# Dealing the work of a fused cross-attention block anew: when one batch ends and the next begins

## The chip, the cores and the metric

The kernel runs on one core of one Trainium2 chip. The metric is the device time of one execution in microseconds (us), and the median of several executions is compared. A profile of one execution gives the rows that are read below; times in it count from the start of its span.

## The reference

For each of 4 batches (512 query rows, 512 context rows, width 512, 16 heads of 32), in float32:

```
x1 = layer_norm(x) * ln1_w + ln1_b
q, k, v = x1 @ q_w + q_b,  ctx @ k_w + k_b,  ctx @ v_w + v_b
a = softmax(q k^T / sqrt(32) + mask) v          # per head
h = a @ cproj_w + cproj_b + x
y = layer_norm(h) * ln2_w + ln2_b
out = h + gelu(y @ fc_w + fc_b) @ proj_w + proj_b   # inner width 2048
```

## The kernel before

**Blocks.** Attention is cut into 16 windows w (batch w // 4, a group of four heads w % 4) and each window into two halves of 256 queries: 32 blocks, numbered p = 2w + half. The same number names the pair (w, half) whose weights block p computes. `block` (L277) does for one block: `scores` (L252: 8 matmuls, one for each head and query tile, into 8 PSUM banks), `soften` (L259: for each of the 8, VectorE adds the mask and takes the minimum, L263, then ScalarE takes the exponential and its sum, L267), four 32x32 transposes by VectorE (`turn`, L275, into the tile tb), and one of the reciprocal sums (L298).

**Copies.** The transposed weights have to change partitions. `copies` (L319) does it with 16 DMAs (L331) of SyncE, whose queue is SP's, from tb to a target: the one tile pT, or gt or xe for the pairs in IN_G (1, 3, 5, 7) and IN_XE (25, 27, 29, 31) while those lie idle. `exchange` (L312) issues them in order of the pairs as soon as the target is free; tb has two buffers.

**Product with V.** `attend` (L334) multiplies by V: 16 small matmuls (L348), then VectorE multiplies by the reciprocal sums into oT (L353), and the target is free again. The table `due` (L1012) says which pairs are attended ahead of each block: mostly pair p - 2 ahead of block p; ahead of block 9 pairs 6 and 7.

**Filling.** TensorE gets other work between the steps of a block. `put(p, ...)` lists it for block p, and `fill(0)`, `fill(1)` and `fill(2)` in `block` run it: the first two run items as long as their given cost fits into one chain (CHAIN, L835), the third runs what is left. Items of cost 0 run along. So the order on every engine is written out by hand in lines 957 to 1010. The items:

- `A(w)`: the chains for k, q and v of window w (L210, L220, L231); each loads the weights of window w + 2 (L208, SP's queue) when its matmuls are issued.
- `inputs(b)`: x1, load x of batch b into four tiles "xn" (L174); x2, its layer norm (`ln1`, L176, in three parts: two of statistics on VectorE, the last of normalization); x3, its four transposes (`ln_turn`, L151); x4, load the context (L169).
- `C(b)`: the output projection c, four chains (L388), each added to the residual by VectorE (L389). The residual of batch 0 stays on the chip.
- `stat`, `rs`, `norm`, `turns2`: statistics (L125), the reciprocal root on GpSimd (L133), normalization (L143 on ScalarE for batch 0 and for x of batches 1 and 2, L147 on VectorE else) and transposes of the second layer norm. For batch 0 the normalized rows go into new "xn" tiles; that pool has four buffers, so x of a batch and the normalized rows of another take turns.
- `some(n)`: the next n chains of the MLP of batches 0 and 1. For batch 0 two chains of fc (y @ fc_w) are one item, `fc_by_pair` (L545), 14 matmuls (L497) by a 7-product scheme on sums of blocks; a chain of the last projection (`proj`, L554) has four matmuls (L556) and one add on VectorE (L560). Each frees weight slots, and `load_mlp` (L439) issues the next loads (L446).

PSUM has 8 banks, taken in turn by everything above; a matmul group waits until the bank's former content has been read. After block 31 the remaining chains, the last two products, c of batch 3 and then the MLP of the other batches run (`last_mlps`, L592).

Of the kernel before, what the change touches and what calls it, by code (L numbers as in the profile page):

```python
# [50 lines left out]
def xattn_block(ctx: ExitStack, tc: tile.TileContext, x, encT, mask, q_w, k_w, v_w, c_w, fc_w, p_w, vecs, rows, out):  # L51
# [65 lines left out]
    def acc_tile(name):  # L117
        return banks[-1].tile([P, D], F32, tag="acc", name=name)
# [9 lines left out]
    def ln_rs(key):  # L128

        ve = small.tile([P, NT], F32, tag="ve", name=f"ve{key[0]}_{key[1]}")  # L130
        nc.gpsimd.tensor_scalar(ve, S["mv", key][:, :, 1], EPS, 1.0, ALU.add, ALU.mult)
        rs = small.tile([P, NT], F32, tag="rs", name=f"rs{key[0]}_{key[1]}")
        nc.gpsimd.tensor_tensor(rs, ve, nhalf, ALU.pow)  # L133
        S["rs", key] = rs
        if key in NORM_ACT:
            nm = small.tile([P, NT], F32, tag="nm", name=f"nm{key[0]}_{key[1]}")
            nc.gpsimd.tensor_tensor(nm, S["mv", key][:, :, 0], rs, ALU.mult)
            nc.gpsimd.tensor_scalar(nm, nm, -1.0, 0.0, ALU.mult, ALU.add)
            S["nm", key] = nm
# [70 lines left out]
    def prep_k(w):  # L210
        b, g = divmod(w, NG)
        kT = k_q(w, 0)
        acc = acc_tile(f"acck_{w}")
        for d in range(ND):
            nc.tensor.matmul(acc, S["wk", w][:, d, :], eT[:, d, :], start=(d == 0), stop=(d == ND - 1))  # L215
        load_w(w + 2, names=("wk",))
        nc.scalar.activation(kT, acc, AF.Identity, bias=vec[:, KB + g : KB + g + 1], scale=1.0)
        S["kT", w] = kT

    def prep_q(w):  # L220
        b, g = divmod(w, NG)
        qT = k_q(w, 1)
        acc = acc_tile(f"accq_{w}")
        for d in range(ND):
            nc.tensor.matmul(acc, S["wq", w][:, d, :], xT[:, d, :], start=(d == 0), stop=(d == ND - 1))  # L225
        load_w(w + 2, names=("wq",))

        nc.scalar.activation(qT, acc, AF.Identity, bias=qb[:, g : g + 1], scale=-scale)  # L228
        S["qT", w] = qT

    def prep_v(w):  # L231
        b = w // NG
        v = five.tile([P, NT, P], F32, tag="v", name=f"v_{w}")
        acc = acc_tile(f"accv_{w}")
        for t in range(NT):
            for d in range(ND):
                nc.tensor.matmul(  # L237
                    acc[:, ts(t, P)], eT[:, d, ts(t, P)], S["wv", w][:, d, :],
                    start=(d == 0), stop=(d == ND - 1),
                )  # L240
        load_w(w + 2, names=("wv",))
        nc.scalar.copy(v, acc.rearrange("p (t f) -> p t f", t=NT))  # L242
        S["v", w] = v
        if w:
            v_bias(w)
# [62 lines left out]
    def target(w, half):  # L308
        pair = 2 * w + half
        return "gt" if pair in IN_G else "xe" if pair in IN_XE else "pT"  # L310

    def exchange():  # L312

        while waiting and target(*waiting[0]) not in held:
            w, half = waiting.pop(0)
            held[target(w, half)] = w, half
            copies(w, half)
# [16 lines left out]
    def attend(w, half):  # L334

        b, g = divmod(w, NG)
        if g == 0 and half == 0:
            S["oT", b] = one.tile([P, NG, L], F32, tag="oT", name=f"oT_{b}")
        v, pT = S["v", w], S["pT", w, half]
        av = acc_tile(f"av_{w}_{half}")  # L340
        o = S["oT", b][:, g, ts(half, 2 * P)]
        shape, kw = "p (a i q) -> p a i q", dict(a=2, i=NI)
        pv = pT[:, :, :PW].rearrange("p i (a t h q) -> p t h a i q", a=2, t=NT, h=HG)
        p = [[pv[:, t, h] for h in range(HG)] for t in range(NT)]
        r = pT[:, :, PW:].rearrange("p i (a q) -> p a i q", a=2)
        for t in range(NT):
            for h in range(HG):
                nc.tensor.matmul(  # L348
                    av[ts(h, HD), : 2 * P].rearrange(shape, **kw), v[:, t, ts(h, HD)], p[t][h],
                    start=(t == 0), stop=(t == NT - 1),  # L350
                )
        o, a = o.rearrange(shape, **kw), av[:, : 2 * P].rearrange(shape, **kw)
        nc.vector.tensor_tensor(o, a, r, ALU.mult)  # L353
        del held[target(w, half)]
        exchange()
# [24 lines left out]
    def c_bias(b):  # L380
        for t in range(NT):
            add_row(S["h", b, t], 0)
# [25 lines left out]
    def stat2(b, t):  # L408
        ln_stat((2, b), t, S["h", b, t])

    def norm2(b, t):
        h = S["h", b, t]
        y = tiles.tile([P, D], F32, tag="xn", name=f"xn2_{b}_{t}") if stays(b, t) else h
        S.setdefault(("yn", b), {})[t] = y
        ln_norm((2, b), t, y, h)

    def proj_bias(b):
        for t in range(NT):
            if stays(b, t):
                add_row(S["hid", b, t], 1)  # L420
# [32 lines left out]
    def sub(o, x0, x1, engine=None):  # L453
        (engine or nc.vector).tensor_tensor(o, x0, x1, ALU.subtract)  # L454
# [16 lines left out]
    def y_blocks(b):  # L471
        return [S["yT", b][:, 2 * k : 2 * k + 2, j * HL : (j + 1) * HL] for k in range(2) for j in range(2)]

    def y_sums(b):
        y11, y12, y21, y22 = y_blocks(b)
        e = nc.vector if b else nc.gpsimd
        sub(ys[:, 0], y12, y11)
        sub(ys[:, 1], y22, ys[:, 0])
        sub(y12, y22, y12, e)
        sub(ys[:, 2], y21, ys[:, 1], e)  # L480
# [356 lines left out]
    def do(fn):  # L837
        return [(0.0, fn)]

    def A(w):  # L840
        if w >= NW:
            return []
        return [
            (CHAIN, lambda: prep_k(w)),
            (CHAIN, lambda: prep_q(w)),
            (CHAIN, lambda: prep_v(w)),
        ]

    def C(b):
        return [(CHAIN, lambda t=t: cproj(b, t)) for t in range(NT)]  # L850
# [4 lines left out]
    def turns2(b):  # L855
        return [(TURN, lambda d=d: ln2_turn(b, d)) for d in range(ND)]
# [9 lines left out]
    def inputs(b):  # L866
        ln = [(0.0, lambda part=part: ln1(b, part)) for part in range(3)]
        return do(lambda: load_x(b)), ln, turns1(b), do(lambda: load_enc(b))
# [36 lines left out]
    x1, x2, x3, x4 = inputs(1)  # L905
# [14 lines left out]
    def some(n):  # L920
        taken = []
        while n > 0:
            n -= 1 if mlp[0][0] == CHAIN else 2
            taken.append(mlp.pop(0))
        assert n == 0
        return taken
# [4 lines left out]
    def h_(b, *ts_):  # L931
        return do(lambda: load_h(b, *ts_))

    def cb(b):
        return do(lambda: c_bias(b))

    def pb_(b):
        return do(lambda: proj_bias(b))

    def rs(b):  # L940
        return do(lambda: ln_rs((2, b)))

    def stat(b, *ts_):
        return do(lambda: [stat2(b, t) for t in ts_])

    def norm(b, *ts_):
        return do(lambda: [norm2(b, t) for t in ts_])
# [3 lines left out]
    def put(p, *work, before=()):  # L951

        work = [item for part in work for item in part]
        ahead[p] = list(before)
        fills[p] = work
# [5 lines left out]
    k6, q6, v6 = A(6)  # L961
# [4 lines left out]
    put(4, x3[:2], [k5], x3[2:])  # L966
    put(5, [v5, q4])
    put(6, [q5, k6])
    put(7, [v6, q6], cb(0))

    x1, x2, x3, x4 = inputs(2)
    k, q, v = A(7)
    c, t2 = C(0), turns2(0)
    put(8, x1, [k, q, v], x2[:1], x4)
    put(9, c[:1], x2[1:2], c[1:2], x2[2:], stat(0, 0), c[2:3], stat(0, 1), c[3:], stat(0, 2, 3), rs(0))
    k, q, v = A(8)
    put(10, [k], do(fc_sums), x3, [v], t2, do(lambda: y_sums(0)), [q], before=norm(0, 0, 1, 2, 3))
    put(11, some(2), pb_(0), some(2))

    k, q, v = A(9)  # L980
    x1, x2, x3, x4 = inputs(3)
    put(12, [k, q], some(2))
    put(13, some(2), [v], x1)
    k, q, v = A(10)
    put(14, [k, q], x2[:1], some(2))
    put(15, x2[1:2], some(2), [v])

    k, q, v = A(11)
    put(16, h_(1, 0, 1), x2[2:], [k, q], x3[:2], some(2), x3[2:3])
    put(17, [v], x3[3:], h_(1, 2, 3), x4, cb(1), C(1))  # L990
    k, q, v = A(12)
    put(18, [q], some(2), [k])
    put(19, some(2), [v])
    k, q, v = A(13)
    put(20, [k, q], some(2))
    put(21, some(2), [v])
    k, q, v = A(14)
    t2 = turns2(1)
    put(22, [k, q], stat(1, 0, 1, 2, 3), rs(1), some(2), norm(1, 0, 1, 2, 3))
    put(23, some(1), [v], t2, pb_(1), some(1), h_(2, 2, 3, 0, 1))  # L1000
    k, q, v = A(15)
    c = C(2)
    put(24, [k, q], cb(2), [v])
    put(25, c)
    put(26, some(2))
    put(27, some(3))
    put(28, some(3))
    put(29, some(3))
# [1 line left out]
    put(31, some(3))  # L1010

    due = {p: (p - 2,) for p in range(10, 2 * NW)}  # L1012
    due |= {p: (p - 3,) for p in range(3, 9)} | {9: (6, 7)}
    for p in range(2 * NW):
        w, half = divmod(p, 2)
        if half == 0 and w and w % NG == 0:
# [23 lines left out]
    c = C(B - 1)  # L1040
# [49 lines left out]
```

## Time and profile before

| | us |
|---|---|
| median of 3 runs | 802.29 |
| lowest and highest | 801.79, 803.43 |
| the profiled execution | 800.17 |
| its span, first to last instruction | 798.2 |
| TensorE busy in it | 779.3 |
| VectorE, ScalarE, GpSimd busy | 614.2, 331.7, 145.1 |

In the rows PE is TensorE's matmul, DVE is VectorE, ACT ScalarE, POOL GpSimd, SPq the DMA-issuing queue of SyncE. A row of the timeline has start, length, engine, line, operation, out<-in, how many instructions were merged, and in brackets the idle time before it and what ended it. On PE each float32 matmul shows as two instructions, so a chain of 4 has x8. Blocks start with their scores (L257): block 8 at 115.94, block 9 at 136.70, block 10 at 155.41, block 11 at 180.64, block 16 at 262.78, block 26 at 433.72, block 28 at 463.09.

### The profile page before, as it was taken

The numbers are of one execution on the slowest core, as the hardware profiler recorded it, in microseconds if no ns is written. First come the engines' busy times: TensorE is split into PE (matmuls) and PEld (weight loads), VectorE is DVE, ScalarE is ACT, GpSimd is POOL, SyncE is SP. The second block draws the span as 40 slices with busy tenths as digits, with TensorE's granted clock in tenths as the row PEclk, the third lists the DMA queues.
The fourth block names the chain that finished last, engine by engine and source line by source line (L and its number), as shares of the span: only waits on it lengthen the run. The fifth ranks groups of instructions, "written<-read, shape, count | busy, mean of one in ns | idle before, by whom it ended". The sixth has DMA issues, their size and how long they took to land.

```text
span 798.2 us, 12709 instructions
## 1 busy us (share of the span) xinstructions
PE 779.3 (98%) x4394; PEld 514.0 (64%) x4394; DVE 614.2 (77%) x1252; ACT 331.7 (42%) x750; POOL 145.1 (18%) x163
## 2 busy tenths in 40 slices
PE   9999998989999999999999989999999999999998
PEld 6555554456665655556654344445888889988897
DVE  3789895958797966769967958838787999779863
ACT  2577753475773545547544457600310321012200
POOL 1210021235120040100231000120041004400052
PEclk9999999989999999999999999999999999999999
DMA  9988889646797876688668789784442330022001
GB/s 331 295 247 239 218 232 258 185 120 179 198 238 178 253 218 183 165 219 207 163 158 242 201 236 229 205 247 142 159 159 84 94 123 18 28 80 80 14 14 40
DMA packets 60960, 137.20 MB, mean 172 GB/s; under 512 B 12464, under 2 KB 15664, under 8 KB 60768
## 3 DMA queue, kind: packets, MB, share of 16 engines
q1 hardware_dynamic: 59472, 132.43, 60.2%
q0 software_dynamic: 896, 2.82, 1.1%
q10 hardware_dynamic: 528, 1.14, 0.6%
q8 instruction: 35, 0.57, 0.3%
q14 instruction: 29, 0.24, 0.1%
HBM read 58.22 MB, written 6.82 MB: 81 GB/s over the span
## 4 chain that ended last, share of the span: by engine, by line
PE 74%; SPq 10%; DVE 9%; DMA 2%; issue 2%; ACT 2%; DVEq 0%; ACTq 0%
PE q L497 17%; SPq L331 9%; PE accp L556 9%; PE r L645 7%; PE accc L388 7%; PE av L348 6%; PE sc L257 6%; PE acck L215 5%; PE accq L225 4%; PE accf L538 3%; PE accv L237 3%; DVE ptt L263 3%; PE q4p L682 2%; DVE tb L275 2%; PE tp L156 1%
## 5 line engine op out<-in xcount | busy, mean ns | idle before, releaser
L267 ACT ACTIVATE ptt<-ptt,mn 128x512 f32<-128x512 f32 x256 | 181.6, 710 | 138.5 <-DVE mn L263 138.3
L263 DVE CUSTOM_DVE_ANT_0 ptt<-sc,mb 128x512 f32<-128x512 f32 x256 | 161.5, 687 | 22.4 <-PE sc L257 17.7
L275 DVE STREAM_TRANSPOSE tb<-ptt 128x1024 f32<-128x1024 f32 x128 | 154.7, 1220 | 10.8 <-ACT ptt L267 8.7
L556 PE MATMUL accp<-pbt,gt 128*128 128x512 f32 x192 | 85.3, 597 | 0.0
L497 PE MATMUL q<-yT,gt 128*128 128x256 f32 x320 | 79.0, 380 | 0.8 <-DVE pbt L389 0.8
L257 PE MATMUL sc<-pbt 32*128 32x512 f32 x512 | 74.4, 625 | 1.4 <-ACT pbt L228 0.8
L497 PEld LDWEIGHTS q<-yT,gt 128*128 128x128 f32 x320 | 60.8, 190 | 9.7 <-DVE pbt L389 1.6
L556 PEld LDWEIGHTS accp<-pbt,gt 128*128 128x128 f32 x192 | 35.7, 190 | 47.2 <-issue 40.3
L237 PEld LDWEIGHTS accv<-ptt,xe 128*128 128x128 f32 x512 | 59.1, 192 | 7.7 <-issue 3.3
L515 ACT ACTIVATE ga<-ga,vec 128x512 f32<-128x512 f32 x40 | 26.7, 714 | 88.4 <-DVE ga L457 88.4
L497 PE MATMUL q<-ys,gt 128*128 128x256 f32 x240 | 61.7, 380 | 0.0
L237 PE MATMUL accv<-ptt,xe 128*128 128x128 f32 x512 | 60.1, 276 | 0.4 <-DMA ptt<-v_w_dram 0.4
L225 PE MATMUL accq<-xe,ptt 128*128 128x512 f32 x128 | 59.0, 604 | 0.0
L215 PE MATMUL acck<-xe,ptt 128*128 128x512 f32 x128 | 58.7, 602 | 0.0
L388 PE MATMUL accc<-wc,oT 128*128 128x512 f32 x128 | 55.8, 594 | 0.0
L249 POOL TENSOR_TENSOR v<-v,row 128x512 f32<-128x512 f32 x16 | 20.4, 1275 | 178.8 <-ACT v L242 178.8
L348 PE MATMUL av<-pT,v 128*32 128x256 f32 x768 | 46.4, 382 | 5.7 <-DMA xe<-tb 3.0
L257 PEld LDWEIGHTS sc<-pbt 32*128 32x128 f32 x512 | 28.6, 188 | 34.7 <-issue 20.0
L497 PEld LDWEIGHTS q<-ys,gt 128*128 128x128 f32 x240 | 45.6, 190 | 6.5 <-DVE gt L454 0.4
L267 ACT ACTIVATION_READ_ACCUMULATOR ptt<-ptt,mn 128x1 f32 x256 | 47.8, 187 | 0.0
L388 PEld LDWEIGHTS accc<-wc,oT 128*128 128x128 f32 x128 | 24.1, 190 | 30.7 <-issue 27.7
L225 PEld LDWEIGHTS accq<-xe,ptt 128*128 128x128 f32 x128 | 24.2, 195 | 30.4 <-issue 25.7
(180 smaller groups left out, 1094.8 us busy)
## 6 DMA issues: line engine op xcount, KB each, us to landing
pT<-tb SPq DMA_DIRECT2D x384, 136.0 KB, 2.4
pbt<-p_w_dram SPq DMA_DIRECT2D x40, 256.0 KB, 3.5
gt<-fc_w_dram SPq DMA_DIRECT2D x40, 256.0 KB, 2.6
gt<-tb SPq DMA_DIRECT2D x64, 136.0 KB, 2.9
xe<-tb SPq DMA_DIRECT2D x56, 136.0 KB, 2.5
pbt<-fc_w_dram SPq DMA_DIRECT2D x24, 256.0 KB, 3.6
ptt<-k_w_dram SPq DMA_DIRECT2D x16, 256.0 KB, 3.7
xe<-encT_dram SPq DMA_DIRECT2D x16, 256.0 KB, 5.2
```

The source lines that it names most:

```text
L215: nc.tensor.matmul(acc, S["wk", w][:, d, :], eT[:, d, :], start=(d == 0), stop=(d == ND - 1))
L225: nc.tensor.matmul(acc, S["wq", w][:, d, :], xT[:, d, :], start=(d == 0), stop=(d == ND - 1))
L237: nc.tensor.matmul(acc[:, ts(t, P)], eT[:, d, ts(t, P)], S["wv", w][:, d, :], start=(d == 0), stop=(d == ND - 1),)
L257: nc.tensor.matmul(S["sc", w, qt][h], qT[r, ts(qt, P)], kT[r, :], start=True, stop=True)
L263: nc.vector.tensor_tensor_reduce(out=s, in0=S["sc", w, qt][h], in1=S["mb", w // NG], scale=1.0, scalar=FMAX, op0=ALU.add, op1=ALU.min, acc ...
L267: nc.scalar.activation(s, s, AF.Exp, bias=mn, scale=-1.0, accum_out=S["sums", w][:, qt, h : h + 1])
L275: nc.vector.transpose(tv[:, qt % 2, 2 * k : 2 * k + 2], S["ps", w, qt, k])
L331: q.dma_start(out=pT[ts(j, HD), i], in_=tb[ts(i, HD), j])
L348: nc.tensor.matmul(av[ts(h, HD), : 2 * P].rearrange(shape, **kw), v[:, t, ts(h, HD)], p[t][h], start=(t == 0), stop=(t == NT - 1),)
L388: nc.tensor.matmul(acc, S["oT", b][:, g, ts(t, P)], wc[:, g, :], start=(g == 0), stop=(g == NG - 1))
L497: nc.tensor.matmul(o, x[:, k], y[:, k], start=(k == 0), stop=(k == 1))
L556: nc.tensor.matmul(acc, gT[q % 2][:, k, ts(t, P)], S["pw", b, q * FQ + k], start=(k == 0), stop=(k == FQ - 1))
```

## The change

The work stays the same; it is moved between blocks 7 and 26 and the end of attention.

- x of batch 2 is loaded at the end of block 7's work (was at the start of block 8's).
- The product of pair 7, the last of batch 0, is no longer due ahead of block 9; it stands inside block 9, behind v of window 7 (moved there from block 8), the context load and the statistics of x.
- The transposes of x of batch 2 move from block 10 into block 9, between the third and the fourth chain of c. The normalization of batch 0 moves from ahead of block 10 to behind its chains for k and v.
- The first fc pair stands in block 11 behind k and v of window 9, not two pairs alone; blocks 12 to 15 share out q, k and v and the MLP anew. The sum of MLP chains up to block 25 is the same.
- The statistics of batch 1 move from block 22 to blocks 20 and 21, and half of its normalization ahead of the fc pair in block 22.
- Block 26 takes three MLP chains instead of two, so one chain less is left for the end.

```diff
-    put(7, [v6, q6], cb(0))
-
     x1, x2, x3, x4 = inputs(2)
     k, q, v = A(7)
     c, t2 = C(0), turns2(0)
-    put(8, x1, [k, q, v], x2[:1], x4)
-    put(9, c[:1], x2[1:2], c[1:2], x2[2:], stat(0, 0), c[2:3], stat(0, 1), c[3:], stat(0, 2, 3), rs(0))
+    put(7, [v6, q6], cb(0), x1)
+    put(8, [k, q])
+    put(9, [v], x4, x2[:2], do(lambda: attend(3, 1)), c[:1], x2[2:], stat(0, 0), c[1:2], stat(0, 1),
+        c[2:3], stat(0, 2), x3, c[3:], stat(0, 3), rs(0))
     k, q, v = A(8)
-    put(10, [k], do(fc_sums), x3, [v], t2, do(lambda: y_sums(0)), [q], before=norm(0, 0, 1, 2, 3))
-    put(11, some(2), pb_(0), some(2))
-
+    put(10, [k, v], norm(0, 0, 1, 2, 3), do(fc_sums), [q], t2, do(lambda: y_sums(0)))
     k, q, v = A(9)
+    put(11, [k, v], some(2), pb_(0))
+
+    put(12, [q], some(2))
     x1, x2, x3, x4 = inputs(3)
-    put(12, [k, q], some(2))
-    put(13, some(2), [v], x1)
     k, q, v = A(10)
-    put(14, [k, q], x2[:1], some(2))
-    put(15, x2[1:2], some(2), [v])
+    put(13, [k], some(2), [v], x1)
+    put(14, [q], x2[:1], some(2))
+    put(15, some(2), x2[1:2], some(2))
...
-    put(20, [k, q], some(2))
-    put(21, some(2), [v])
+    put(20, [k, q], some(2), stat(1, 0, 1))
+    put(21, some(2), [v], stat(1, 2, 3), rs(1))
     k, q, v = A(14)
     t2 = turns2(1)
-    put(22, [k, q], stat(1, 0, 1, 2, 3), rs(1), some(2), norm(1, 0, 1, 2, 3))
+    put(22, [k, q], norm(1, 0, 1), some(2), norm(1, 2, 3))
...
-    put(26, some(2))
+    put(26, some(3))
...
-    due |= {p: (p - 3,) for p in range(3, 9)} | {9: (6, 7)}
+    due |= {p: (p - 3,) for p in range(3, 9)} | {9: (6,)}
```

## Prediction, on record before the changed kernel ran

> **What bounds the kernel now.** I read the page first, then the stretches of the kernel one by one, then TensorE's instructions in order of time.
>
> ```profile
> PE 779.3 (98%) x4394; PEld 514.0 (64%) x4394; DVE 614.2 (77%) x1252; ACT 331.7 (42%) x750; POOL 145.1 (18%) x163
> ...
> DMA packets 60960, 137.20 MB, mean 172 GB/s; under 512 B 12464, under 2 KB 15664, under 8 KB 60768
> ```
>
> TensorE is busy 98% of the span, so only its idle time, and time in which its matmuls run long, can be won. The view of stretches (PE busy comes first, the granted clock third from the end) shows where that is:
>
> ```profile
> 129.75:139.61 9.86, 7.37 (x81) 3.37 (x81) 3.08 (x9) 0.65 (x2) 1.27 (x1) 0.83 0.90 264
> 155.41:180.64 25.23, 21.75 (x133) 13.77 (x129) 14.56 (x29) 14.62 (x30) 11.38 (x15) 0.86 0.47 119
> 180.64:262.78 82.14, 80.40 (x485) 49.97 (x481) 68.17 (x144) 48.74 (x109) 20.35 (x26) 1.00 0.79 200
> 433.72:463.09 29.37, 26.33 (x140) 11.30 (x137) 23.78 (x51) 12.53 (x34) 1.62 (x3) 1.00 0.82 223
> ```
>
> Two stretches also lose clock. 9.86 us at a mean clock of 0.83 lose 1.7 us and 25.23 us at 0.86 lose 3.5 us, beside 2.5, 3.5, 1.7 and 3.0 us without a matmul in the four. TensorE's rows (start, length, line, and in brackets the idle time before it):
>
> ```profile
> 126.09 3.73 PE L237 MATMUL accv<-ptt,xe 128*128 128x128 f32 x32
> 129.75 1.94 PE L348 MATMUL av<-pT,v 128*32 128x256 f32 x32
> 134.18 2.59 PE L348 MATMUL av<-gt,v 128*32 128x256 f32 x32 [2.49 <-DMA gt<-tb]
> 136.70 2.98 PE L257 MATMUL sc<-pbt 32*128 32x512 f32 x16
> 155.41 2.56 PE L257 MATMUL sc<-pbt 32*128 32x512 f32 x16
> 161.44 1.91 PE L156 MATMUL tp<-ident,xn 128*128 128x128 f32 x16
> 163.19 3.74 PE L237 MATMUL accv<-ptt,xe 128*128 128x128 f32 x32
> 169.75 1.94 PE L156 MATMUL tp<-ident,xn 128*128 128x128 f32 x8 [2.83 <-DVE mn L263]
> 172.34 2.09 PE L156 MATMUL tp<-ident,xn 128*128 128x128 f32 x8 [0.65 <-ACT pbt L217]
> 174.22 4.62 PE L225 MATMUL accq<-xe,ptt 128*128 128x512 f32 x8
> 178.77 1.93 PE L348 MATMUL av<-pT,v 128*32 128x256 f32 x32
> ```
>
> Unhurried work, for the sizes of things:
>
> ```profile
> 203.54 3.60 PE L225 MATMUL accq<-xe,ptt 128*128 128x512 f32 x8
> 206.97 1.89 PE L497 MATMUL q<-yT,pbt 128*128 128x256 f32 x8
> 213.11 1.93 PE L348 MATMUL av<-pT,v 128*32 128x256 f32 x32
> 214.97 2.00 PE L257 MATMUL sc<-pbt 32*128 32x512 f32 x16
> 227.48 1.93 PE L348 MATMUL av<-pT,v 128*32 128x256 f32 x32 [0.70 <-DMA pT<-tb]
> ```
>
> From start to start a chain for q takes 3.43, one fc pair 6.14, a product with V 1.86, scores 1.9 (their 2.00 less the overlap that the other rows have), a chain for v 3.7 (126.09 to 129.75) and 16 transposes 1.75 (161.44 to 163.19). I use 3.5 for a chain of k or of the projections.
>
> **The change, part by part.** *Block 10.* Before, the norms of batch 0 go to ScalarE ahead of the block's exponentials, into tiles that batch 2 still holds until it is transposed:
>
> ```profile
> 163.14 2.93 ACT L143 ACTIVATE xn<-h,nm,rs 128x512 f32<-128x512 f32 x4 [10.82 <-PE tp L156]
> ```
>
> They wait 10.82 us, all exponentials behind them, VectorE behind those, and at last the PSUM banks that the next transposes need: hence the 2.83 us at 169.75 and the slow clock. From 163.19 to 178.77 are 15.6 us for v, 16 transposes and q, worth 3.7 + 1.75 + 3.43 = 8.9: **6.7 us lost**. After, the order of instructions has batch 2's transposes in block 9 and the norms behind block 10's exponentials, k and v. The norms need 2.9 us on ScalarE, which q's 3.43 covers with half a microsecond to spare; if that cover is gone, the transposes wait for the rest, 2.4 us at most. I charge 0.2. The scores at 155.41 ran 0.6 long because VectorE came late from the layer norm's sums; after, it has caught up by then. Together **7.1 gained**.
>
> *Block 9.* Before, the last product of batch 0 follows pair 6's at once and waits 2.49 us for its 16 copies; with the slow clock, 129.75 to 139.61 loses 9.86 - 2 x 1.86 - 1.9 = **4.2 us**. After, k and q end at 126.1, pair 6's product at 128.0, the scores at 129.9 or about 0.5 later (VectorE finishes block 8 at 129.0 and only then frees the last bank), v at 134.1. There the product waits for the same copies. But x of batch 2 is now loaded ahead of them:
>
> ```profile
> 120.73 0.53 SPq L208 DMA_DIRECT2D ptt<-v_w_dram  x1
> 121.85 10.26 SPq L331 DMA_DIRECT2D gt<-tb  x16
> 132.22 1.97 SPq L174 DMA_DIRECT2D xn<-x_dram  x4
> 128.59 0.40 DVE L298 STREAM_TRANSPOSE tb<-rr 128x256 f32<-128x256 f32 x1
> ```
>
> Nothing on SP's queue stood idle there, so the four loads push the copies back by at least their issue, 1.97 us: product at 136.2. The upper end is the other place where the trace has a weight load, x and 16 copies in that order:
>
> ```profile
> 215.56 10.04 SPq L331 DMA_DIRECT2D pT<-tb  x16
> 226.81 0.38 SPq L208 DMA_DIRECT2D ptt<-v_w_dram  x1
> 227.28 1.80 SPq L174 DMA_DIRECT2D xn<-x_dram  x4
> 230.60 11.87 SPq L331 DMA_DIRECT2D pT<-tb  x16
> ```
>
> From 226.81 to the last issue at 242.47 are 15.7 us, and the last copy lands some 2.1 us after its issue (132.11 to 134.18): 17.7. From 120.73 that gives 138.4, and 139.1 with the second weight load that stands here. I take 137.3, between the ends. The wait is then 3.2 us (2.1 to 5.0) instead of 2.5. A wait of that length may cost the clock again, 1.7 us by the first stretch above; a wait that ends at 461.23 shows 3.01 us and clock 1.00, so I charge 1.0. 4.2 - 3.2 - 0.5 - 1.0 = **0.5 lost**.
>
> The Trainium skill (TensorE: Matmul & The Clock Gate, "HAM oscillation — how this bites in real kernels") gives the rule that PE gaps up to about 3.4 us keep the clock. By it this charge would be nothing and the part 0.5 gained. The trace disagrees: after 2.49 and 2.83 us the clock was lost.
>
> *Moved on PE in block 9:* c's first two chains read pair 6's half alone; the third reads pair 7's in its last step, some 10 us after the product. Until then VectorE has the rest of half a block and four stats (3.2 us by the row at 376.72 below) ahead of its multiply; c's first two chains cover that, and what it is later than they are would be idle time. load_enc now follows pair 8's copies; it needs block 10's k, over 10 us later.
>
> *Blocks 11 to 15* have the same chains, dealt anew. The work: five products and scores 18.8, two chains each for k, q and v 21.3, four fc pairs 24.6, four projection chains 14.1, together 78.8 us in the 82.14 of the third stretch, 3.4 lost. After, blocks 12 and 14 hold only q and an fc pair: 1.86 + 1.9 + 3.43 + 6.14 = 13.3 us. There is one pT buffer: copies start when the product before has freed it, and the next product waits for them. Block 13 of before shows that circle at its shortest: 213.11 to 227.48, 14.37 us, with 0.70 idle. So block 12 waits about **1.0**. In block 14 x of batch 3 stands ahead of the copies again: 17.7 us from v's load, issued as v ends, where TensorE needs 13.3: 4.4 waited. At the other end, with the loads landing unseen, the copies need 11.9 from their start (215.56 to 227.48), 2.3 after v: 0.9. I take **2.6**, and 0.9 for the clock; another 0.3 for scores that wait for VectorE. Before hid these loads under k, q and two projection chains. 3.4 - 4.8 = **1.4 lost**.
>
> *Stats of batch 1* go from block 22 to 20 and 21:
>
> ```profile
> 365.06 1.94 PE L348 MATMUL av<-pT,v 128*32 128x256 f32 x32 [0.84 <-DVE tb L275]
> 376.72 0.65 DVE L125 BATCH_NORM_STATS2 st<-h 128x6 f32<-128x512 f32 x1
> 384.09 1.99 PE L257 MATMUL sc<-pbt 32*128 32x512 f32 x14
> 386.26 1.12 PE L257 MATMUL sc<-pbt 32*128 32x512 f32 x2 [0.18 <-DVE oT L353]
> ```
>
> Block 21 is one in which VectorE is late already (0.84 idle). Two stats, 1.7 us of VectorE, go straight onto that (the two at the end of block 20 stand after its last add, in a block of 17 us with room); block 23's scores get back what stats and norms in block 22 cost them: 384.09 to 387.38 are 3.3 us for 1.9 or 2.0, 1.3 too many. **0.4 lost** (0 to 2).
>
> *Block 26* gets a third chain:
>
> ```profile
> 433.72 2.00 PE L257 MATMUL sc<-pbt 32*128 32x512 f32 x16
> 445.84 0.40 DVE L298 STREAM_TRANSPOSE tb<-rr 128x256 f32<-128x256 f32 x1
> 447.65 10.57 PE L556 MATMUL accp<-pbt,gt 128*128 128x512 f32 x24
> 461.23 1.93 PE L348 MATMUL av<-pT,v 128*32 128x256 f32 x32 [3.01 <-DMA xe<-tb]
> ```
>
> Pair 26's copies start when VectorE ends the block, 446.2, whatever TensorE does; its product waits until 461.23. With one chain more (10.57/3 = 3.5) TensorE arrives at 461 instead of 458. The wait goes and a chain is done that stood at the very end: **3.5 gained**. *The end* then has one chain less ahead of the last c:
>
> ```profile
> 553.52 0.69 DVE L389 TENSOR_TENSOR pbt<-accc,pbt 128x512 f32<-128x512 f32 x1 [2.67 <-PE accc L388]
> ```
>
> VectorE has 2.67 us of slack there and loses 3.5: it becomes the one that is late, by about 0.5 with the moved add off its list. **0.5 lost** (0 to 1.5).
>
> Sum: 7.1 - 0.5 - 1.4 - 0.4 + 3.5 - 0.5 = **7.8 us gained**. The profiled execution took 800.17 (span 798.2), 2.1 under the median of the runs, 802.29; I take the gain off the median: **794.5**.
>
> **The rivals.** *No new clock loss* (17%): if the moved waits fall across windows as the one at 461.23 did, 1.9 us come back: **792.6**. For: that row. Against: two of three waits over 2.4 us were hit. The Trainium skill's rule above would give the same time. *Loads hidden* (12%): both lower ends, waits of 2.1 and 0.9, and no clock charge: 1.1 + 1.7 + 1.9 = 4.7 better, **789.8**. Against: DMA share 0.90 in the first stretch. *The norms still wait* (5%), on x of batch 2 or late stats, so block 10 keeps its loss: 7.1 less gained, **801.6**, no change. Against: in the new order the transposes stand a block ahead. *Slower* (10%): the x loads set both waits at the page's mean DMA rate. Four tiles of 512 x 128 numbers of 4 bytes, 1.05 MB, at 172 GB/s are 6.1 us, so block 9's product waits 6.2 and block 14's 7.0, each with two windows of half clock (3.4): 5.4 and 6.9 worse than forecast, **806.8**. Against: 17.7 us for load, x and copies at 226.81. It decides from about 4 us beyond my value at both places.
>
> **How the numbers follow.** Forecast 56%, around 794.5 (790.5 to 799). A measurement of this kernel tells about 0.2%, 1.6 us, from no change. Faster: 56 + 17 + 12 = 85%, less 2 for the upper tail of the forecast: 0.83. Same: the 5 of that rival and 1 of the tail, 0.06. Slower: 10 and 1 of the tail, 0.11. Range 788.5 to 801.5: it leaves out the slower case, half of the unchanged one and a little below.
>
> **What would show it.** Right: ScalarE's norms of batch 0 without a wait, no idle before the transposes of block 10, and under 0.7 us of idle before block 28's product; still 2 to 5 us before pair 7's product, and new idle of 1 and about 2.6 us before the products at the ends of blocks 12 and 14. Wrong: pair 7's product starting later than 139, a wait at the transposes before block 11, more than 1.5 us idle before the first fc pair after c, or another clock loss where none is charged.

## The result and the profile after

| us | before | changed |
|---|---|---|
| median | 802.04 (4 runs) | 796.92 (4 runs) |
| lowest and highest | 801.44, 803.43 | 796.58, 797.56 |
| the profiled execution | 800.17 | 797.24 |
| its span | 798.2 | 795.4 |

The ratio is 0.9935, with a 95% interval of 0.9917 to 0.9952: 5.1 us gained by the medians, 2.9 by the two profiled executions (2.8 by their spans). The forecast was 7.8 us and 794.5.

The changed kernel's view of stretches, for block 9 from its scores on, block 10, blocks 11 to 15, and block 26 up to block 28's product (PE busy first; third from the end the granted clock, the share of its full speed that TensorE's clock had):

```profile
128.88:162.67 33.79, 28.13 (x164) 15.28 (x160) 20.78 (x46) 12.45 (x26) 2.88 (x5) 0.90 0.70 187
162.67:178.85 16.18, 16.18 (x116) 10.09 (x113) 13.08 (x26) 12.18 (x26) 7.64 (x12) 1.00 0.75 187
178.85:263.23 84.38, 79.57 (x485) 49.49 (x481) 68.70 (x146) 51.26 (x111) 24.65 (x29) 1.00 0.78 200
434.07:461.13 27.06, 26.78 (x116) 11.47 (x113) 24.22 (x52) 12.52 (x34) 1.63 (x3) 1.00 0.78 211
```

Block 10 has no idle time and no lowered clock left, and block 26 only 0.28 us. Block 9 carries the loss: 5.66 us without a matmul, and a mean clock of 0.90. TensorE's rows show the same (start, length, line, in brackets the idle time before and what ended it):

```profile
131.12 3.84 PE L237 MATMUL accv<-ptt,xe 128*128 128x128 f32 x32
140.62 3.64 PE L348 MATMUL av<-gt,v 128*32 128x256 f32 x32 [5.66 <-DMA gt<-tb]
144.19 11.51 PE L388 MATMUL accc<-wc,oT 128*128 128x512 f32 x24
155.53 1.91 PE L156 MATMUL tp<-ident,xn 128*128 128x128 f32 x16
...
171.71 3.60 PE L225 MATMUL accq<-xe,ptt 128*128 128x512 f32 x8
175.15 1.91 PE L156 MATMUL tp<-ident,xn 128*128 128x128 f32 x16
...
209.51 1.93 PE L348 MATMUL av<-pT,v 128*32 128x256 f32 x32 [1.26 <-DMA ptt<-q_w_dram]
...
243.64 1.93 PE L348 MATMUL av<-pT,v 128*32 128x256 f32 x32 [3.55 <-DMA ptt<-q_w_dram]
...
461.13 1.93 PE L348 MATMUL av<-pT,v 128*32 128x256 f32 x32 [0.28 <-DVE tb L298]
...
551.79 1.99 PE L497 MATMUL q<-yT,gt 128*128 128x256 f32 x8 [1.83 <-DVE pbt L389]
```

Pair 7's product starts at 140.62, after a wait of 5.66 us, and takes 3.64 us where 1.93 is its length at full clock; c's first three chains take 11.51 for 10.57. In block 10 the transposes at 175.15 follow q at once. The new waits at the ends of blocks 12 and 14 are 1.26 and 3.55 us, and behind the second the product still took 1.93. Block 28's product waits 0.28 instead of 3.01. The first fc pair of the end waits 1.83 instead of 0.78.

ScalarE's norms of batch 0 (count, shortest, median and longest in ns, first and last start), and then the two groups of SyncE's queue that stand ahead of pair 7's product:

```profile
L143 ACT ACTIVATE xn<-h,nm,rs x4: 801/802/815, 172.4 to 174.5; 128x512 f32<-128x512 f32 x4
```

```profile
122.54 2.72 SPq L174 DMA_DIRECT2D xn<-x_dram  x4
125.35 13.23 SPq L331 DMA_DIRECT2D gt<-tb  x16
```

The norms start at 172.4 and run one after the other. The four loads of x take 2.72 us to issue, and then the 16 copies take 13.23 us where the kernel before took 10.26.

### The profile page after: what moved, and what is told of

Read it like the earlier page. It is cut to its first block, busy times and chain, and to the rows that moved or that the text cites. A ratio compares the mean times of both kernels' runs of the same rounds, so it can differ in the third digit from the quotient of the medians.

```text
span 795.4 us, 12699 instructions
## 1 busy us (share of the span) xinstructions
PE 775.2 (97%) x4394; PEld 511.0 (64%) x4394; DVE 614.7 (77%) x1252; ACT 334.2 (42%) x752; POOL 145.8 (18%) x163
## 4 chain that ended last, share of the span: by engine, by line
PE 84%; DMA 5%; DVE 4%; SPq 4%; issue 1%; ACT 1%; POOL 0%; DVEq 0%; POOLq 0%
PE q L497 20%; PE accp L556 9%; PE r L645 7%; PE sc L257 6%; PE av L348 6%; PE acck L215 6%; PE accv L237 6%; PE accc L388 5%; PE accq L225 5%; PE accf L538 4%; SPq L331 3%; PE q4p L682 2%; PE q1p L700 2%; PE tp L156 2%; DMA gt<-tb 1%
## 5 line engine op out<-in xcount | busy, mean ns | idle before, releaser
L257 PE MATMUL sc<-pbt 32*128 32x512 f32 x512 | 70.9, 615 | 1.5 <-ACT pbt L228 0.8
L215 PEld LDWEIGHTS acck<-xe,ptt 128*128 128x128 f32 x128 | 23.3, 192 | 32.7 <-issue 23.4
```

The costliest lines, as they stand in the source:

```text
L257: nc.tensor.matmul(S["sc", w, qt][h], qT[r, ts(qt, P)], kT[r, :], start=True, stop=True)
```

## The experiments

Each kernel was timed beside the kernel before on the same chip (the table has both medians). Its ratio to before is given with its 95% interval; 0.0035 of it is 2.8 us. One execution of each is profiled, and stretches of it are measured from the start of one block's scores to another's. "End" is from block 31's scores to the end of the last busy instruction.

| kernel | median, of before | ratio to before | blocks 8, 9 | block 10 | 11 to 15 | 16 to 22 | 23 to 27 | end |
|---|---|---|---|---|---|---|---|---|
| before | | 1 | 39.46 | 25.23 | 82.14 | 121.31 | 79.00 | 289.47 |
| changed | 796.92, 802.04 | 0.9935 (0.9917 to 0.9952) | 45.92 | 16.18 | 84.38 | 122.51 | 77.26 | 286.79 |
| e1 norms' place alone | 796.34, 802.73 | 0.9917 (0.9886 to 0.9948) | 39.31 | 18.97 | 82.37 | 120.91 | 80.43 | 289.83 |
| e2 norms ahead again | 794.99, 802.73 | 0.9914 (0.9885 to 0.9944) | 43.55 | 16.18 | 82.76 | 122.51 | 77.12 | 289.26 |
| e3 x of batch 2 behind | 789.63, 802.73 | 0.9841 (0.9806 to 0.9876) | 38.49 | 16.18 | 84.52 | 122.51 | 76.95 | 288.82 |
| e4 dealt as before | 793.85, 802.73 | 0.9899 (0.9867 to 0.9932) | 44.66 | 16.22 | 81.73 | 122.60 | 76.91 | 287.81 |
| e5 third chain alone | 798.93, 800.57 | 0.9968 (0.9941 to 0.9995) | 42.66 | 25.05 | 82.91 | 121.00 | 78.23 | 287.47 |
| e6 product after c | 793.77, 800.57 | 0.9902 (0.9870 to 0.9935) | 39.92 | 16.18 | 85.42 | 122.51 | 76.99 | 287.98 |
| e7 e3 and e4 | 788.04, 800.57 | 0.9839 (0.9804 to 0.9873) | 37.46 | 16.18 | 82.17 | 122.51 | 76.91 | 289.41 |
| e8 both x behind | 787.45, 800.57 | 0.9825 (0.9793 to 0.9857) | 37.68 | 16.18 | 81.92 | 122.51 | 77.22 | 289.23 |
| e9 x by GpSimd | 795.68, 800.41 | 0.9940 (0.9917 to 0.9963) | 43.44 | 16.18 | 85.05 | 122.74 | 77.13 | 287.63 |
| e10 e8, end's order | 788.63, 800.41 | 0.9843 (0.9816 to 0.9870) | 38.89 | 16.18 | 81.90 | 122.51 | 76.91 | 290.06 |
| e11 e8, statistics back | 788.19, 800.41 | 0.9840 (0.9806 to 0.9874) | 37.34 | 16.18 | 81.42 | 120.92 | 78.60 | 287.83 |
| e12 e8, sums late | 785.97, 801.96 | 0.9810 (0.9775 to 0.9845) | 37.49 | 16.18 | 81.94 | 122.51 | 77.34 | 286.52 |

My theory is the forecast's: each loss is a wait at one place, the waits add up, and the loads of x delay the copies by their place in SyncE's queue. The main rivals: a wait that is removed comes back elsewhere, and it is not the place but something that both places share.

**e1 and e2: what cost block 10, the norms' place or the shared tiles?** e1 is the kernel before with

```diff
-    put(10, [k], do(fc_sums), x3, [v], t2, do(lambda: y_sums(0)), [q], before=norm(0, 0, 1, 2, 3))
+    put(10, [k], do(fc_sums), x3, [v], norm(0, 0, 1, 2, 3), [q], t2, do(lambda: y_sums(0)))
```

> The kernel before, with one line changed: the norms of batch 0 stand behind block 10's chains for k and v and its transposes of x of batch 2, so behind the block's exponentials on ScalarE; the four tiles are still shared by x of batch 2 and the norms. Theory (what cost block 10 was the place in ScalarE's queue, 10.82 us of waiting with all exponentials behind it): block 10 shrinks from 25.2 us to 18 to 19, no idle before its later transposes, about 6.5 us faster than before, near 795.5. Rival (the shared tiles make the wait, wherever the norms stand): the norms still wait for the transposes, batch 0's transposes wait for the norms, and the time is within 2 us of before, 800 or more.

Block 10 fell from 25.23 to 18.97 us. TensorE's rows of e1, from q on, and its product of block 28:

```profile
166.80 3.60 PE L225 MATMUL accq<-xe,ptt 128*128 128x512 f32 x8
...
170.96 1.64 PE L156 MATMUL tp<-ident,xn 128*128 128x128 f32 x13 [0.23 <-ACT xn L143]
...
174.39 2.00 PE L257 MATMUL sc<-pbt 32*128 32x512 f32 x16
...
454.73 3.44 PE L348 MATMUL av<-pT,v 128*32 128x256 f32 x32 [2.90 <-DMA xe<-tb]
```

The idle 2.83 us is gone and q takes 3.60 instead of 4.62; only 0.23 us of waiting for the norms is left. The theory holds: with the tiles still shared, the place in ScalarE's queue alone frees 6.3 of the 7.3 us. The last row belongs to a later section. e2 is the changed kernel with

```diff
-    put(10, [k, v], norm(0, 0, 1, 2, 3), do(fc_sums), [q], t2, do(lambda: y_sums(0)))
+    put(10, [k, v], do(fc_sums), [q], t2, do(lambda: y_sums(0)), before=norm(0, 0, 1, 2, 3))
```

> The changed kernel, with the norms of batch 0 put back ahead of block 10's exponentials; the tiles are free by then, as batch 2's transposes stay in block 9. Theory (a place ahead of the exponentials costs only what the norms wait there): they wait for the last statistics and the reciprocal root of block 9, about 1 to 2 us, and take 2.9 us, so the exponentials start 3 to 5 us late; TensorE has k, v and q to do, and loses 0 to 2 us at the next scores or transposes: 797 to 799. Rival (the shared tiles were all of it): the same as the changed kernel, 796.9 within 0.7. Second rival (the place was all of it): block 10 loses 5 us or more again, 802.

e2's norms on ScalarE, and the transposes that need them:

```profile
L143 ACT ACTIVATE xn<-h,nm,rs x4: 799/800/814, 160.5 to 162.7; 128x512 f32<-128x512 f32 x4
```

```profile
171.10 1.91 PE L156 MATMUL tp<-ident,xn 128*128 128x128 f32 x16
```

They start at 160.5, 1.9 us after the block's scores (9.7 in the changed kernel), and block 10 takes the same 16.18. The loss of 0 to 2 us that my theory expected did not come, and by the trace the first rival is right: with free tiles the place costs nothing. By the ratios e2 and the changed kernel can't be told apart; what lies between their profiles is mostly blocks 8 and 9, where the code is the same (43.55 and 45.92 us). Either remedy is nearly enough: without its 1.75 us of transposes, e1's block 10 is 1.0 us longer than the changed kernel's. The stall needed both: a queue in strict order and, at its head, work that waits for tiles. The changed kernel applies both, and one line would have had nearly the whole gain of block 10; e1's ratio is no worse than that of the whole change.

**e3, e6 and e9: what cost block 9?** e3 is the changed kernel with the loads of x of batch 2 behind pair 7's copies in SyncE's queue.

```diff
-    put(7, [v6, q6], cb(0), x1)
-    put(8, [k, q])
+    put(7, [v6, q6], cb(0))
+    put(8, x1, [k, q])
```

> The changed kernel, with the four loads of x of batch 2 issued at the start of block 8's work, behind pair 7's copies on SP's queue, as before. Theory (the loads delay pair 7's copies: the product of pair 7 waited 5.66 us and ran with a lowered clock after it): the wait falls to under 1.5 us and the 3.64 us product to 1.9, block 9 loses 2 to 3 us instead of 8.8, unless x comes late for its statistics (0.5 to 1.5): about 6 us faster than the changed kernel, near 791. Rival (the copies are held by the issue of the DMA queue alone, or by the weight loads beside them): the wait stays near 5 us, 796 to 797.

SyncE's queue and TensorE's rows of e3:

```profile
123.02 10.31 SPq L331 DMA_DIRECT2D gt<-tb  x16
133.43 1.96 SPq L174 DMA_DIRECT2D xn<-x_dram  x4
...
135.84 1.93 PE L348 MATMUL av<-gt,v 128*32 128x256 f32 x32 [0.40 <-issue]
137.70 10.57 PE L388 MATMUL accc<-wc,oT 128*128 128x512 f32 x24
```

The copies take 10.31 us again, the wait is 0.40, the product 1.93 and the chains 10.57. Blocks 8 and 9 take 38.49 us, 7.4 less than in the changed kernel, and the ratio says 7.5 us. The theory holds: the early loads cost more than the change as a whole won. In all six kernels with this block 9 and x behind the copies (e3, e7, e8, e10 to e12) the wait is under 1 us; in the four with the loads ahead and the product at the same place (changed, e2, e4, e9) it is 3.65 us or more. e9 asks why, and leaves the order of the copies as in e3 while x is loaded at the early time, by another engine:

```diff
-            queue(b).dma_start(out=S["xn", b][t], in_=x[b, ts(t, P), :])
+            (nc.gpsimd if b == 2 else queue(b)).dma_start(out=S["xn", b][t], in_=x[b, ts(t, P), :])
```

> The changed kernel, with the four loads of x of batch 2 issued by GpSimd at the same time (about 122 us) instead of by SyncE ahead of pair 7's copies. Theory (it is the place in SyncE's queue that delays the copies: the loads' own issue of 2 to 3 us and the copies behind them held until loads have landed): the copies start near 122.5 and land by 136, the wait ahead of pair 7's product is under 2 us and the product takes 1.9: block 9 loses 2 to 4 us, 790 to 792. Rival (the DMA engines carry the loads and the copies at the same time, and the bytes set the pace whoever issues them): the wait stays at 3.5 us or more with the lowered clock, 795 to 797.

GpSimd's and SyncE's issues and the product in e9; then, from the view of DMAs (119 to 143 us), copies and loads with the median us from issue to landing in e9 and in e3:

```profile
121.67 2.21 POOL L174 DMA_DIRECT2D xn<-x_dram  x4
...
122.75 12.89 SPq L331 DMA_DIRECT2D gt<-tb  x16
...
138.89 3.59 PE L348 MATMUL av<-gt,v 128*32 128x256 f32 x32 [3.75 <-DMA ptt<-k_w_dram]
```

```profile
gt<-tb SPq DMA_DIRECT2D x16, 136.0 KB, 5.7
...
xn<-x_dram POOLq DMA_DIRECT2D x4, 256.0 KB, 6.1
```

```profile
gt<-tb SPq DMA_DIRECT2D x16, 136.0 KB, 3.7
...
xn<-x_dram SPq DMA_DIRECT2D x4, 256.0 KB, 3.6
```

The copies are issued from 122.75, as early as in e3, and yet the product waits 3.75 us and the clock falls; the ratio, from 12 executions, is near that of the changed kernel (0.9940 and 0.9935) and far from e3's (0.9841). My theory is refuted: the delay comes without the place in SyncE's queue.

In e9 the copies need 5.7 us to land instead of 3.7. In the changed kernel the same delay shows elsewhere, for there, in the same view, the copies land fast once they are issued:

```profile
gt<-tb SPq DMA_DIRECT2D x16, 136.0 KB, 2.7
```

It is their issue that is held. SyncE's DMAs take eight semaphores in turn, so each waits until the one eight before it has landed: by the trace's DMA records the fourth copy starts at 128.69, when the weights issued at 122.07 have landed (128.68). What the two kernels share is the bytes. From the issue of the load of v's weights (121.42 in the changed kernel) to the landing of the last copy, the same records show 16.9 to 19.0 us in the five profiles with early loads (16.94 in e9, 16.93 in e2) and 13.1 to 14.6 in the nine others. The first is for 3.80 MB (two weight loads of 0.26, x 1.05, 16 copies of 136 KB 2.23), the second for 2.75 MB: 189 to 225 GB/s in all 14. So loads issued ahead delay the copies whichever of the two engines issues them; more semaphores were not tried. The Trainium skill (DMA: Bandwidth & Descriptors, "Issuing engines are not separate DMA queues") says so: DMAs from all issuing engines run on the same 16 DMA engines and interleave. This run agrees, by 5.7 us against 3.7.

e6 leaves the loads where they are and fills the wait:

```diff
-    put(9, [v], x4, x2[:2], do(lambda: attend(3, 1)), c[:1], x2[2:], stat(0, 0), c[1:2], stat(0, 1),
+    put(9, [v], x4, x2[:2], c[:1], do(lambda: attend(3, 1)), x2[2:], stat(0, 0), c[1:2], stat(0, 1),
```

> The changed kernel, with the product of pair 7 one chain of c later, so that the first chain of c (3.5 us of matmuls, which read pair 6's half alone) stands in its wait; x stays ahead of the copies. Theory (the wait for the copies of pair 7 is the cost, 5.66 us, and the lowered clock follows from its length): about 2.1 us of wait are left and the clock stays at 1.00, so 3.5 from the wait and 2 to 2.7 from the clock, 5 to 6 us faster than the changed kernel, near 791.5. Rival (the clock is lowered by the wait whatever its length is, from 2.1 us on): 3.5 faster, 793.4. Second rival (c's later chains then wait for the product's multiply on VectorE): 0 to 2 faster.

TensorE's rows of e6:

```profile
135.56 3.60 PE L388 MATMUL accc<-wc,oT 128*128 128x512 f32 x8
140.96 1.93 PE L348 MATMUL av<-gt,v 128*32 128x256 f32 x32 [1.81 <-DMA gt<-tb]
...
150.13 1.13 PE L388 MATMUL accc<-wc,oT 128*128 128x512 f32 x2 [1.03 <-DVE oT L353]
```

The copies land as late as before (140.96 beside 140.62), 1.81 us of wait are left, and the product takes 1.93: the clock stayed. That separates the two costs. From the product's start to block 10's scores are 17.73 us instead of 22.05: 3.5 for the chain that now stands ahead, 2.6 for the clock (1.71 of the product and 0.94 of the chains), less 1.3 of new short waits and 0.5 of longer steps beside them. The row at 150.13 shows the larger wait, 1.03 us for VectorE's multiply of the product, as the second rival had it. That the clock stayed is a single case: of the waits of 1.5 to 2.5 us, 7 of 16 lost it (last section). By the ratio e6 gains 2.7 us over the changed kernel, with intervals that overlap, and not the 5 to 6 of the theory. By the trace blocks 8 and 9 are 6.0 us shorter, but blocks 11 to 15 and the end are 2.2 longer; a wait of 2.99 us in block 14 that lost the clock, and one of 2.49 instead of 1.83 ahead of the first fc pair, are part of it.

**e4, e7 and e8: what cost blocks 11 to 15?** e4 is the changed kernel with these blocks dealt as before.

```diff
-    put(11, [k, v], some(2), pb_(0))
+    put(11, some(2), pb_(0), some(2))
-    put(12, [q], some(2))
+    put(12, [k, q], some(2))
+    put(13, some(2), [v], x1)
...
-    put(13, [k], some(2), [v], x1)
-    put(14, [q], x2[:1], some(2))
-    put(15, some(2), x2[1:2], some(2))
+    put(14, [k, q], x2[:1], some(2))
+    put(15, x2[1:2], some(2), [v])
```

> The changed kernel, with blocks 11 to 15 dealt as before: the new waits of 1.26 and 3.55 us for the copies at the ends of blocks 12 and 14 should go, as every block has one or two chains more between its copies and its product. Theory: blocks 11 to 15 go from 84.4 back to about 82.1 us, 2.2 us faster than the changed kernel, near 794.7. Rival (the two waits only take the place of waits that come elsewhere, since the copies of the pairs follow one another in a circle): 796 to 797.5.

e4's stretch of blocks 11 to 15, and the longest wait in it:

```profile
175.16:256.89 81.73, 80.79 (x484) 50.12 (x480) 68.85 (x146) 48.76 (x109) 24.26 (x28) 1.00 0.79 202
```

```profile
222.29 1.93 PE L348 MATMUL av<-pT,v 128*32 128x256 f32 x32 [0.76 <-DMA pT<-tb]
```

81.73 instead of 84.38 us: the theory holds in the trace (2.65 us), while the intervals of the ratios overlap. The other profiles agree: with this deal and early loads (changed, e2, e3, e6, e9) these blocks took 82.76 to 85.42 us, dealt as before (before, e1, e4, e5, e7) 81.73 to 82.91. e8 keeps the new deal and moves the loads of x of batch 3 behind the copies, as e3 does for batch 2:

```diff
-    put(13, [k], some(2), [v], x1)
-    put(14, [q], x2[:1], some(2))
-    put(15, some(2), x2[1:2], some(2))
+    put(13, [k], some(2), [v])
+    put(14, x1, [q], some(2))
+    put(15, some(2), x2[:2], some(2))
```

> The changed kernel with both loads of x (batch 2 and batch 3) issued behind the copies of the block before instead of ahead of them; blocks 11 to 15 keep the new deal. Theory: block 9's wait goes as when x of batch 2 alone is moved, and the 3.55 us wait at the end of block 14 falls to about 1 (the copies are still a circle of 14.4 us against 13.3 us of work): 8 to 9 us faster than the changed kernel, near 788.5. Rival (block 14 waits because the block is short, not because of the loads): no faster than with x of batch 2 alone, near 791.

e8's stretch of blocks 11 to 15, its two waits, and the first fc pair of the end:

```profile
171.01:252.93 81.92, 79.56 (x485) 49.58 (x481) 68.61 (x146) 51.14 (x111) 24.50 (x29) 1.00 0.81 206
```

```profile
201.63 1.93 PE L348 MATMUL av<-pT,v 128*32 128x256 f32 x32 [1.23 <-DVE gt L457]
...
233.34 1.93 PE L348 MATMUL av<-pT,v 128*32 128x256 f32 x32 [1.13 <-DVE gt L457]
...
541.66 3.20 PE L497 MATMUL q<-yT,gt 128*128 128x256 f32 x8 [2.04 <-DVE pbt L389]
```

The wait in block 14 falls from 3.55 to 1.13 us and the five blocks take 81.92 us (81.42 to 81.94 in e10 to e12). By the ratio e8 is 8.8 us faster than the changed kernel, as expected; that it is also faster than e3 (0.9825 beside 0.9841) the intervals don't show. So the new deal costs nothing by itself; it took away the cover under which the loads of x had been hidden. What is left, some 1.2 us in each of the two short blocks, is the circle of copies and products that the forecast reckoned with: the rows name VectorE, but by the trace's DMA records the last copy of the first of them lands at 201.2, half a microsecond ahead of the product, and no load stands between the copies. e7 joins e3 and e4:

> Two edits in one, the changed kernel with x of batch 2 behind pair 7's copies and blocks 11 to 15 dealt as before. Theory (the two costs add up, they lie 40 us apart): 6 and 2.2 us faster than the changed kernel, near 788.7, faster than either edit alone. Rival (one of the two costs is not what it seems): 791 to 796.

Both stretches come out (37.46 and 82.17 us), so the costs add up there by the trace. The ratio doesn't show it: 0.9839 beside e3's 0.9841, with intervals wider than the 2.2 us expected between them. Some of the gain is given back at the end, which took 289.41 us (e3 288.82, changed 286.79). The last row of e8 shows what happens there. The first fc pair waits 2.04 us, and its first matmuls then take 3.20 us instead of 2.0.

**e10 and e12: the end.** Both are e8 with VectorE's list changed between c of batch 3 and the first fc pair. e10:

```diff
-    run(c[:2])
-    p_sums(first_c + 2)
-    run(c[2:])
+    run(c)
+    p_sums(first_c + 2)
```

> The kernel with both loads of x behind the copies, and at the end VectorE's sums of weights for the third fc chain pair moved behind the last two adds of c of batch 3 (2.7 us of VectorE that stood between them). Theory (VectorE's list sets the 2 us wait ahead of the first fc pair of the end, and the lowered clock behind it follows from that wait): the wait falls from 2.0 to about 0.8 and the pair's first matmuls from 3.2 to 2.0 us: 1.2 us, and up to 2.3 more where the clock was lost, 785 to 786.5. Rival (the sums are needed by then, or the adds wait for TensorE's last chain anyway): within 0.5 of 787.4.

TensorE's first two steps of that fc pair in e10:

```profile
539.30 1.99 PE L497 MATMUL q<-yT,gt 128*128 128x256 f32 x8 [0.79 <-DVE pbt L389]
543.15 1.76 PE L497 MATMUL q<-ys,gt 128*128 128x256 f32 x4 [1.86 <-DVE ys L454]
```

The first wait fell to 0.79 as expected, but a second one of 1.86 us came behind it, for the sums of y, which on VectorE stand behind the sums that were moved, and the clock fell all the same: nothing won. The wait had only moved. e12 takes the sums out of this stretch (`p_sums` in the loop behind the second fc pair):

```diff
-    run(c[:2])
-    p_sums(first_c + 2)
-    run(c[2:])
+    run(c)
...
+                if b == SPLIT and c == half + 1:
+                    p_sums(half + 2)
```

> The kernel with both loads of x behind the copies, and at the end VectorE's 2.7 us of sums of projection weights (read only some 20 us later) taken out of the stretch between c of batch 3 and the first fc pairs and put behind the second of these pairs. Theory (the length of VectorE's list, 14 us without a pause, sets the waits ahead of the first matmuls of the first fc pair, wherever in the list the sums stand; when they stood behind c's adds the wait only moved on, 0.79 and 1.86 us): both waits together fall from 2.0 to about 1.3 us and the clock stays at 1.00, 0.7 us, and up to 3 where the clock was lost: 784.5 to 786.5. Rival (the waits here are not what slows these matmuls): within 0.5 of 787.4, with first matmuls still longer than 2.0 us.

The same two steps in e12:

```profile
537.96 1.99 PE L497 MATMUL q<-yT,gt 128*128 128x256 f32 x8 [0.78 <-DVE pbt L389]
539.79 1.03 PE L497 MATMUL q<-ys,gt 128*128 128x256 f32 x4
```

One wait of 0.78 us is left and the clock stays: the end takes 286.52 us, 2.7 less than e8's. The theory holds in the trace; the ratios of e12 and e8 (0.9810 and 0.9825) have intervals that overlap. e12 has the lowest ratio found (785.97 us beside 801.96), and its interval lies below that of the changed kernel, 0.9935.

**e5: the third chain in block 26 alone,** in the kernel before.

```diff
-    put(26, some(2))
+    put(26, some(3))
```

> The kernel before, with three chains of the MLP in block 26 instead of two and nothing else. Theory: the 3.01 us wait for pair 26's copies goes and a chain is done that stood at the end; block 26 to 28 gains 3.5 to 4.0, the end gives back 0.5 to 1.1 as the first fc pair there waits for VectorE's adds: 2.5 to 3.4 us faster, 798.6 to 799.5. Rival (the time is given back at the end, where VectorE sets the pace): within 1 us of before, 801 to 802.5.

TensorE's rows of e5 at block 9's product and at the first fc pair of the end:

```profile
139.07 3.64 PE L348 MATMUL av<-gt,v 128*32 128x256 f32 x32 [4.79 <-DMA xn<-x_dram]
...
557.56 2.00 PE L497 MATMUL q<-yT,gt 128*128 128x256 f32 x8 [2.28 <-DVE pbt L389]
```

By the ratio it gains 2.6 us of 800.57 (0.4 to 4.7), which doesn't quite shut out the rival. By the trace blocks 23 to 27 are 0.8 us shorter with a chain more in them and the end is 2.0 shorter: 2.8 us, as the theory says, with 1.5 given back where the fc pair waits 2.28 instead of 0.78. The first row is a surprise: this code of block 9 is that of the kernel before, and its wait is 4.79 us instead of 2.49.

**e11: the statistics of batch 1 back in block 22,** in e8.

```diff
-    put(20, [k, q], some(2), stat(1, 0, 1))
-    put(21, some(2), [v], stat(1, 2, 3), rs(1))
+    put(20, [k, q], some(2))
+    put(21, some(2), [v])
...
-    put(22, [k, q], norm(1, 0, 1), some(2), norm(1, 2, 3))
+    put(22, [k, q], stat(1, 0, 1, 2, 3), rs(1), some(2), norm(1, 0, 1, 2, 3))
```

> The kernel with both loads of x behind the copies, and the statistics and the normalization of batch 1 in blocks 20 to 22 as in the kernel before. Theory (the statistics in block 21 cost 1.1 us ahead of the product of pair 20's successor and 1.2 of longer scores, and give back 1.0 in block 23): blocks 16 to 22 shrink by 1.2 us and blocks 23 to 27 grow by 0.8 to 1.0; the time moves by 0.2 to 0.4, within 0.5 of 787.4. Rival (one of the two sides is not real): blocks 16 to 27 together differ by more than 1 us from those of the same kernel with the statistics moved.

Blocks 16 to 22 are 1.6 us shorter and blocks 23 to 27 1.4 us longer: 0.2 us between them. Theory as expected; this part of the change neither wins nor loses anything that can be told.

## Why the prediction was right, and where it was wrong

The sign was right and the time, 796.9, lies within the range. Every term but the small one of the statistics has the sign forecast; one was mis-sized badly. Gains and losses in us, the measured ones from the two profiled executions:

| term | forecast | measured | from |
|---|---|---|---|
| block 10 | +7.1 | +7.3 | 25.23 - 16.18, less 1.75 of transposes moved to block 9 |
| block 9 | -0.5 | -4.7 | 39.46 + 1.75 - 45.92 for blocks 8 and 9 |
| blocks 11 to 15 | -1.4 | -2.2 | 82.14 - 84.38 |
| statistics of batch 1 | -0.4 | +0.1 | blocks 16 to 25: 170.94 - 170.84 |
| block 26 | +3.5 | +3.9 | blocks 26, 27: 29.37 - 28.93, and 3.5 of chain |
| end | -0.5 | -0.8 | 289.47 - 286.79 is 2.7 of the 3.5 |
| ahead of block 8 | 0 | -0.8 | 115.94 and 116.75; unchanged work (114.29 to 118.77 in the 14 profiles) |
| sum | +7.8 | +2.8 | spans 798.2 and 795.4 |

*Block 10* was right in size, and for the reason given: no wait at the norms, no idle time before the transposes. What I did not see is that either half of the edit does it (e1, e2).

*Block 9* is the step that failed, at "I take 137.3, between the ends". The product started at 140.62, beyond the 139 that the forecast had set as its mark, and its wait of 5.66 us is beyond my upper end of 5.0. The lower end priced the loads of x by what they take to issue, 1.97 us. That price is the error: e9 shows that the issue isn't the price, the bytes are. The upper end came from another place, where one weight load, x and 16 copies, 3.54 MB, took 17.45 us by the DMA records, or 203 GB/s; it put the product 18.4 us behind the first weight load, and the product came 19.2 behind it (121.42 to 140.62). Taking the middle of a wrong price and a nearly right one lost 2.5 us of the 4.2 that these two profiles lie apart from the forecast. The price of the slower rival, 1.05 MB at the mean DMA rate and so a wait of 6.2 us, was the nearer one here. It did not decide, since in block 14 the wait was 3.55 and not 7.0. The charge for the clock, 1.0, lay between two cases; the clock was lost, for 2.65 us, which is 1.65 more of the 4.2.

*Blocks 11 to 15:* the waits came where I put them, 1.26 us (1.0 forecast) and 3.55 (2.6, up to 4.4). No clock was lost there, against my 0.9, and that was luck: behind this wait in block 14 the clock was lost in e3, e6 and e9 (3.00, 2.99 and 3.02 us) and kept in e2 (2.27 us). The difference between 1.4 and 2.2 is in that second wait and in short ones. That the loads of x are its cause is shown by e8.

*The end* gave back 1.05 us by the rows of the fc pair (0.5 forecast, up to 1.5). In later kernels the same wait also cost the clock (e8's end takes 289.23 us, e12's 286.52, of which 1.26 is the wait); I had not thought of that.

*The reference point.* I took the gain off the median, 2.1 us above the profiled execution. Much of that spread lies in block 9: blocks 8 and 9 of the code before took 39.46, 39.31 and 42.66 us in three profiled executions (before, e1, e5), and those of the changed code 45.92, 43.55 and 44.66 (changed, e2, e4). By the means block 9 loses 44.71 - 40.48 - 1.75 = 2.5 us, not 4.7; the sum is then 5.0 us, and the medians say 5.1.

## What to carry to other kernels

When a transfer is moved ahead of others, price it by the bytes that are then in flight ahead of the one waited for (here about 200 GB/s, so by estimate some 5 us for 1.05 MB), not by the time its issue takes, and don't expect another issuing engine to help. When a stall has two causes in series (a strict queue, and at its head work that waits for a buffer), look for the cheaper one to remove: here one line did. A wait that is removed from TensorE's list by reordering another engine's list may only move to the next matmul, so look at the length of that engine's list before its order.

## What the runs showed of the hardware

The clock after a wait isn't a matter of the wait's length alone. Among TensorE's waits of over 1.5 us between block 8 and the first fc pairs of the end, in these 14 profiles, the matmuls behind the wait ran long after 7 of 16 waits of 1.5 to 2.5 us, after 8 of 10 of 2.8 to 3.8 us, and after all 3 of 4.8 to 5.7 us. The same wait at the same place can go either way: ahead of block 28's product 3.01 us kept the clock in the kernel before (1.93 us), and 2.90 us lost it in e1 (3.44 us); at the end of block 14, 3.55 us kept it in the changed kernel, and in e3 3.00 us did not:

```profile
235.08 3.21 PE L348 MATMUL av<-pT,v 128*32 128x256 f32 x32 [3.00 <-DMA ptt<-q_w_dram]
```

The Trainium skill (TensorE: Matmul & The Clock Gate, "HAM oscillation — how this bites in real kernels") puts the limit at gaps of about 3.4 us. The runs disagree: 13 waits below that length lost the clock. By these counts I would now price a wait of 2 to 2.5 us as an even chance, and a longer one as four chances in five or more, of losing 1.3 to 2.6 us more (1.3 behind 3.00 us in e3, 1.5 behind 2.90 us in e1, 2.6 behind 5.66 us in the changed kernel).

Where the copies of pair 7 land differs from execution to execution by more than 2 us with the same code (waits of 2.49, 2.50 and 4.79 in the code before; 5.66, 3.65 and 4.95 in the changed code). What sets that was not tried.
